# x + b_o of a batch by a broadcast of b_o and a transfer that adds x to it, in place of GpSimd's additions

## The chip, the cores and the metric

The kernel runs on one core of a Trainium2 chip. A core has a matrix engine (TensorE, in the profile PE, its weight loads PEld), a vector engine (VectorE, DVE), an activation engine (ScalarE, ACT), a general engine (GpSimd, POOL), a queue engine that only issues transfers (SyncE, SP), and 16 DMA engines. Each engine executes its own instructions in order; semaphores make one wait for another. The metric is the device time of one execution in microseconds; the kernel before takes 791.95 us (median of 3 runs, 791.62 to 792.87).

## The reference

The input x has 16 batches of 512 rows of 256 floats. All arithmetic is float32. One block, attention and then a feed-forward net, each with a residual and a layer norm:

```python
def favor(x):                          # per head of 16 columns
    p = exp(x - max(x)); return p / (sum(p) + 1e-6)
q = favor(split_heads(x @ Wq + bq)); k = favor(split_heads(x @ Wk + bk))
v = split_heads(x @ Wv + bv)
probs = (q @ k.T) / (sum(q) + 1e-6)
attn = merge_heads(probs @ v) @ Wo + bo
x = layernorm(x + attn)

def fp4_linear(x, w): return fp4(x) @ fp4(w).T   # blocks of 16, scale = max|.|/6, 8 magnitudes
h = silu(fp4_linear(x, w_gate)) * fp4_linear(x, w_up)      # 704 columns
out = layernorm(x + fp4_linear(h, w_down))
```

The change concerns one term: the `x + ... + bo` of the first layer norm's argument.

## The kernel before

A batch is four tiles of 128 rows (`TPB = 4`), worked in two pairs of tiles; there are 32 pairs. Attention is linear in k and v: with no softmax over keys, `probs @ v @ Wo` is q times a small matrix, so a batch goes through these steps.

- `load_x` (L394): the batch's x, 512 KB, by SP into a ring of four buffers. The first batch comes in two halves (L400). Right after batch 1's load, SP issues all other weights (`load_rest`, L465 to L475), among them b_o, broadcast to 128 partitions.
- `project`, per pair: PE transposes x (L636), ACT copies the result (L639), PE multiplies by Wq and Wk (L778), DVE adds the bias (L781) and takes the maximum per head (L786), POOL subtracts it (L790).
- `features`, per batch: ACT's exponential (L801), DVE's sums (L803) and reciprocals (L810 to L814), POOL's scaling of the four tiles (L820).
- `key_values`, per batch: DVE sums k (L829), PE multiplies x by k (L836), by Wv (L852, L853) and by Wo (L864), which gives a 256x256 matrix M; ACT copies it (L843, L870).
- `attend`, per pair: PE transposes q (L636), POOL forms `xb = x + b_o` (L885) into a ring of two buffers, PE multiplies q by M (L892). Then `norm`: DVE adds PE's result and xb (L733) and sums, ACT squares (L740, L742), POOL takes the inverse root (L746 to L748), ACT applies (L755). The pair goes to DRAM by ACT's queue (L903).
- `quantise`, `gate_up`, `down`, per pair: the feed-forward net. SP reads the pair back (L910), DVE and ACT make fp4 codes, SP regroups codes and scales through DRAM (L676, L681, L699, L704), POOL multiplies codes by scales (L929, L1009), PE runs the gate and up products (L957) and the down product (L1026), `norm` again, and the output goes by ACT's queue, for the last two pairs by SP's.

The weights of the feed-forward net are quantised by DVE, ACT and POOL (`weight_scales`, `fp4_exact`, L509 to L584) between the attention work of the first batches. `LEAD = 11` makes attention run some 11 batches ahead of the feed-forward net.

Nothing is ordered by hand. Each step is an `op` with an engine, a cost in us, a due time, what it reads and writes, and the ring buffers it takes. `Plan.order` simulates the engines with these costs and emits the steps in the order in which they start there; every engine then executes its instructions in that order, whatever the real times are. Its rule, for one engine:

```python
first = min(t for t, _ in c)
t, o = min(((t, o) for t, o in c if t <= first + 0.02), key=lambda x: (x[1].due, x[1].at))
```

`c` holds the steps that can start, with their earliest start `t`. A step can start when the steps it depends on have ended (0.3 us later, `LAG`, if they are on another engine) and its ring has a free buffer. So a step that can start earlier goes first, and the due time decides among those that can start at practically the same time. A transfer (`dma`) is two steps: the issue on its queue and a step of an engine of its own, `DMA:name`, with the time to landing. An x load costs SP 0.1 there, `load_rest` 0.1; the first x half is given 4.5 us, Wq, Wk and Wv 7.0 us, Wo and b_o 14.0 us from the start. Steps on POOL, and some on DVE, also share one `port` in the plan, one at a time.

Of the kernel before, what the change touches and what calls it, by code (L numbers as in the profile page):

```python
# [14 lines left out]
ALU = mybir.AluOpType  # L15
AX = mybir.AxisListType

P = 128
HD = 16
BLK = 16  # L20

LEAD = 11

FIRST = 2

# [4 lines left out]
PAIR = 25.0  # L30
# [65 lines left out]
class Plan:  # L96
# [7 lines left out]
    def op(self, eng, us, due, fn, ins=(), outs=(), holds=(), table=None, port=None, name=""):  # L104
        o = Op()
        o.eng, o.us, o.fn, o.due, o.table, o.name = eng, us, fn, due, table, name

        o.port = eng == "POOL" if port is None else port
        o.preds, o.succs, o.new, o.bufs, o.end = set(), [], [], [], None
        ins = [x if isinstance(x, tuple) else (x, None) for x in ins]  # L110
        outs = [x if isinstance(x, tuple) else (x, None) for x in outs]
        for b, key in ins:
            for k, w in b.last.items():
                if key is None or k is None or k == key:
                    o.preds.add(w)
        for b, key in outs:
            if b not in o.new:
                o.new.append(b)
            for k, w in b.last.items():
                if key is None or k is None or k == key:  # L120
                    o.preds.add(w)
            for k, rs in b.reads.items():
                if key is None or k is None or k == key:
                    o.preds.update(rs)
        for b, key in ins:
            b.reads.setdefault(key, []).append(o)
        for b, key in outs:
            b.last[key] = o
            b.reads[key] = []
        for b in holds:  # L130
            if b not in o.new:
                o.new.append(b)
        for b in {id(b): b for b in [b for b, _ in ins + outs] + list(holds)}.values():
            b.users += 1
            o.bufs.append(b)
        o.preds.discard(o)
        for p in o.preds:
            p.succs.append(o)
        o.left = len(o.preds)
        o.at = len(self.ops)  # L140
        self.ops.append(o)
        return o
# [103 lines left out]
def t_pe(n):  # L246
    return 2 * (n / 1200.0 + 0.002)
# [19 lines left out]
def tile_favor_fp4_block(  # L267
# [16 lines left out]
    nc = tc.nc  # L284
    B, L, D = hidden.shape
    FF = w_gate.shape[0]
    TPB = L // P
# [30 lines left out]
    op = plan.op  # L318

    def buf(shape, tag, bufs, name, dtype=F32):  # L320
        return Buf(sb, [P] + list(shape), tag, bufs, name, dtype)

    def dma(name, us, due, fn, ins=(), outs=(), queue="SP", issue=0.45, holds=()):

        op(queue, issue, due, fn, ins=ins, outs=outs, holds=holds)
        op("DMA:" + name, us, due, lambda: None, ins=ins, outs=outs)
# [4 lines left out]
    def psum(tag, name):  # L331
        return Bank(share, tag, name)
# [38 lines left out]
    def twice(ap):  # L371

        return ap.unsqueeze(1).to_broadcast([ap.shape[0], 2, ap.shape[1]])
# [9 lines left out]
    def pu(ap):  # L383

        return ap.rearrange("p (u d) -> p u d", u=2)
# [26 lines left out]
    b_o = const.tile([P, D], F32, name="b_o")  # L412
# [27 lines left out]
    def loaded(name, at):  # L440
        b = Fixed(name)
        op("DMA:" + name, at, 0.0, lambda: None, outs=[b])
        return b

    wqkv_in, wo_in = (loaded(n, t) for n, t in (("wqkv", 7.0), ("wo", 14.0)))
# [183 lines left out]
    def transposed(srcs, tag, name, due, src_ins, bufs=2):  # L629

        pt = psum("pt", f"p{name}")
        dst = buf([4, P], tag, bufs, name)

        def tr():
            for j, s in enumerate(srcs()):
                nc.tensor.transpose(pt[:, j, :], s, ident)  # L636

        op("PE", 2 * t_pe(P), due, tr, ins=src_ins, outs=[pt], holds=[dst], name=name)
        op("ACT", t_act(4 * P), due, lambda: nc.scalar.copy(dst.tile, pt.tile), ins=[pt], outs=[dst])  # L639
        return dst  # L640
# [118 lines left out]
        op("ACT", 0.6 * n, due, apply, ins=[(r, key), nb, rstd], outs=[(dst, key)])  # L759


    qks, Ms = {}, {}

    def project(b, p, due):

# [110 lines left out]
    def attend(b, p, due):  # L876
        i = b * PPB + p
        two = slice(2 * p, 2 * p + 2)
        x, qk, M = xs[b], qks[b], Ms[b]
        qT = transposed(  # L880
            lambda: [qk[:, 2 * p + u, c * P : (c + 1) * P] for u in range(2) for c in range(DC)],
            "qT", f"qT_{i}", due, [(qk, 2 * p), (qk, 2 * p + 1)],
        )
        xb = buf([2, D], "xb", 2, f"xb_{i}")
        op("POOL", 1.4, due, lambda: nc.gpsimd.tensor_tensor(xb.tile, x[:, two, :], twice(b_o), ALU.add),  # L885
           ins=[x, wo_in], outs=[xb])
        pa = psum("pm", f"pa_{i}")

        def mm_a():
            for u in range(2):  # L890
                for c in range(DC):
                    nc.tensor.matmul(  # L892
                        pu(pa.tile)[:, u, :], qT[:, 2 * u + c, :], M[:, c, :],
                        start=c == 0, stop=c == DC - 1,
                    )

        r = buf([2, D], "r", 3, f"r1_{i}")
        op("PE", 2 * DC * t_pe(D), due, mm_a, ins=[qT, M], outs=[pa], holds=[r, xb], name="attend")
        x1 = buf([2, D], "x1n", 2, f"x1n_{i}")
        norm(pa, lambda u: xb[:, u, :], x1, f"a{i}", due, [xb], r, lambda u: x1[:, u, :])  # L900

        d = Buf(dr, [P, 2, D], "x1", NP, f"dx1_{i}")
        dma(f"wx1_{i}", 3.0, due, lambda: nc.scalar.dma_start(d.tile, x1.tile), ins=[x1], outs=[d], queue="ACT")  # L903
        st[i] = {"d": d}
# [136 lines left out]
    def due_at(j):  # L1041

        return (j - PPB * LEAD) * PAIR

    T0 = 0.0
    for b in range(B):
        d = due_at(PPB * b)
        load_x(b, d - 6 * PAIR)
        for p in range(PPB):
            project(b, p, d + (p - 3) * PAIR)  # L1050
        features(b, d - PAIR)
        key_values(b, d - 0.8 * PAIR)
        for p in range(PPB):
            attend(b, p, d + (p - 0.5) * PAIR)
# [63 lines left out]
```

## Time and profile before

| | |
|---|---|
| median of 3 runs | 791.95 us (791.62 to 792.87) |
| the profiled execution, its own time | 793.69 us |
| its span in the profile | 792.0 us |
| mean granted clock of PE | 0.995 |
| PE busy | 768.6 us, 97% |
| DVE, POOL, ACT busy | 656.7 us, 455.9 us, 416.5 us |
| DMA packets | 89.23 MB, mean 113 GB/s |
| L885, the additions | 32, mean 1285 ns, 41.0 us, from 15.8 to 392.9 us |

Busy time is what an engine's instructions cover; an instruction that starts before the one ahead of it has ended is counted once. A row of a timeline has the start and the duration in us, engine, line, operation, output and inputs, shapes and count; a bracket at its end gives the idle time before it and what ended that. A list of waits has who waited for whom, the total in us, how many times, and the longest. In the table by stretch, a row has the window, its length, each engine's busy time with the number of instructions, PE's granted clock, the share of the DMA engines' time, and GB/s.

### The profile page before, as it was taken

How to read it: one execution, taken by the hardware profiler on the slowest of the kernel's cores; microseconds unless marked ns; L12 is line 12 of the kernel's file. 1: busy time of each engine (PE TensorE's matmuls, PEld its weight loads, DVE VectorE, ACT ScalarE, POOL GpSimd, SP SyncE). 2: the span in 40 equal slices, each digit the busy share in tenths (PEclk: the TensorE clock that was granted, in tenths of full speed). 3: DMA queues.
4: the chain of work that ended last, by engine and by line, in shares of the span. 5: the costliest groups of instructions: out<-in, count | busy, mean ns of one | idle time of the engine just before them, and what ended most of it. 6: DMA issues, size and time to landing. Idle time of an engine off the chain costs nothing.

```text
span 792.0 us, 10915 instructions
## 1 busy us (share of the span) xinstructions
PE 768.6 (97%) x3118; PEld 552.5 (70%) x3118; DVE 656.7 (83%) x1340; ACT 416.5 (53%) x893; POOL 455.9 (58%) x602
## 2 busy tenths in 40 slices
PE   7999999989998999999999999999999999999996
PEld 3567657657676777767777777777777777777774
DVE  2998999999888798697697798888878988778784
ACT  2347766868887783544545444444334444344441
POOL 5668788889887755574554435434533543543633
PEclk9999999999999999999999999999999999999998
DMA  9112411211111044404335454554554554464441
GB/s 277 45 55 86 142 53 54 82 60 62 54 53 62 30 129 133 118 37 124 100 112 138 145 171 136 152 149 134 149 154 135 145 149 140 125 179 129 136 130 41
DMA packets 104348, 89.23 MB, mean 113 GB/s; under 512 B 44512, under 2 KB 87904, under 8 KB 104288
## 3 DMA queue, kind: packets, MB, share of 16 engines
q1 hardware_dynamic: 90704, 71.49, 31.8%
q10 hardware_dynamic: 13584, 17.04, 6.0%
q8 instruction: 25, 0.41, 0.2%
q14 instruction: 35, 0.29, 0.1%
HBM read 53.28 MB, written 35.21 MB: 112 GB/s over the span
## 4 chain that ended last, share of the span: by engine, by line
PE 62%; DVE 12%; DMA 8%; POOL 8%; issue 4%; ACT 4%; SPq 2%; ACTq 0%; POOLq 0%; DVEq 0%
PE bank L957 26%; PE bank L1026 14%; PE bank L778 8%; PE bank L892 5%; PE bank L836 5%; POOL hq L1009 3%; DMA out_dram<-y 3%; DVE qk L781 2%; PE bank L636 2%; DVE mx L786 2%; DMA hcT<-g_h 2%; SPq L681 1%; POOL xqT L929 1%; DVE fs L803 1%; PE bank L852 1%
## 5 line engine op out<-in xcount | busy, mean ns | idle before, releaser
L957 PE MATMUL bank<-w_guT,xqT 128*128 128x352 f32 x1024 | 311.3, 459 | 0.0
L957 PEld LDWEIGHTS bank<-w_guT,xqT 128*128 128x128 f32 x1024 | 193.8, 190 | 100.4 <-ACT g L962 0.2
L1009 POOL TENSOR_TENSOR hq<-hcT,hq 128x384 f32<-128x384 bf16 x124 | 127.3, 1058 | 179.3 <-DMA hcT<-g_h 101.4
L1026 PE MATMUL bank<-w_dT,hq 128*128 128x256 f32 (+1 forms) x768 | 173.1, 379 | 1.1 <-DVE r L718 1.1
L1026 PEld LDWEIGHTS bank<-w_dT,hq 128*128 128x128 f32 (+1 forms) x768 | 144.9, 190 | 27.5 <-issue 1.9
L778 PE MATMUL bank<-w_qkv,xT 128*128 128x512 f32 x256 | 120.8, 602 | 3.8 <-DVE qk L781 1.9
L964 DVE TENSOR_TENSOR h<-bank,g 128x352 f32<-128x352 f32 x128 | 65.7, 515 | 50.9 <-ACT g L962 24.1
L962 ACT ACTIVATE g<-bank 128x352 f32<-128x352 f32 x128 | 57.6, 458 | 87.7 <-PE bank L957 77.8
L666 ACT ACTIVATE sq<-h,magic 128x704 f32<-128x704 uint16 x64 | 56.2, 878 | 79.2 <-DVE h L663 78.6
L820 POOL TENSOR_TENSOR qk<-qk,fr 128x512 f32<-128x512 f32 x64 | 67.0, 1073 | 20.5 <-DVE fr L814 18.9
L790 POOL TENSOR_TENSOR qk<-qk,mx 128x512 f32<-128x512 f32 x64 | 67.4, 1068 | 19.2 <-DVE mx L786 19.0
L778 PEld LDWEIGHTS bank<-w_qkv,xT 128*128 128x128 f32 x256 | 46.6, 193 | 45.4 <-issue 35.8
L755 ACT ACTIVATE y<-r,nb_d,rstd_d 128x256 f32<-128x256 f32 x60 | 32.6, 591 | 59.2 <-POOL nb_d L748 59.2
L929 POOL TENSOR_TENSOR xqT<-xcT,xs 128x256 f32<-128x256 bf16 x64 | 46.3, 740 | 27.6 <-DMA d_h<-sT_h 23.4
L836 PE MATMUL bank<-qk,x 128*128 128x256 f32 x256 | 59.7, 387 | 2.1 <-ACT qT L639 2.1
L892 PE MATMUL bank<-M,qT 128*128 128x256 f32 x256 | 59.6, 381 | 1.8 <-ACT M L870 1.8
L655 DVE TENSOR_REDUCE bank<-h 128x44 f32<-128x704 f32 x64 | 57.1, 893 | 1.6
L663 DVE SCALAR_TENSOR_TENSOR h<-h,bank 128x704 f32<-128x704 f32 x64 | 56.7, 886 | 2.1
L836 PEld LDWEIGHTS bank<-qk,x 128*128 128x128 f32 x256 | 49.5, 195 | 12.7 <-ACT qT L639 3.4
L781 DVE TENSOR_TENSOR qk<-bank,b_qkv 128x512 f32<-128x512 f32 x64 | 43.0, 681 | 18.3 <-PE bank L778 17.9
L892 PEld LDWEIGHTS bank<-M,qT 128*128 128x128 f32 x256 | 47.8, 190 | 13.2 <-ACT M L870 3.8
L885 POOL TENSOR_TENSOR xb<-x,b_o 128x512 f32<-128x512 f32 x32 | 41.0, 1285 | 22.8 <-DVE r L733 22.7
(137 smaller groups left out, 1083.3 us busy)
## 6 DMA issues: line engine op xcount, KB each, us to landing
g_h<-hw SPq DMA_DIRECT2D x31, 384.0 KB, 2.8
hcT<-g_h SPq DMA_DIRECT2D x124, 96.0 KB, 2.4
hq<-d_h SPq DMA_DIRECT2D x31, 384.0 KB, 4.1
dx<-x1n ACTq DMA_DIRECT2D x32, 256.0 KB, 2.0
x<-dx SPq DMA_DIRECT2D x32, 256.0 KB, 3.1
x<-_attn_hidden_states_dram SPq DMA_DIRECT2D x15, 512.0 KB, 3.5
out_dram<-y ACTq DMA_DIRECT2D x30, 256.0 KB, 3.3
xs<-d_x SPq DMA_DIRECT2D x32, 128.0 KB, 2.5
```

The lines of the kernel that those rows point to most:

```text
L655: op("DVE", t_dve(n), due, lambda: nc.vector.tensor_reduce(amax[:, g], b3(src()), AX.X, ALU.max, apply_absolute_value=True), ins=[src_b], ...
L778: op("PE", t_pe(D2), due, lambda c=c, u=u, pqk=pqk: nc.tensor.matmul(pqk.tile, xT[:, 2 * c + u, :], w_qkv[:, c, :D2], start=c == 0, stop=c ...
L781: op("DVE", t_dve(D2), due, lambda t=t, pqk=pqk: nc.vector.tensor_tensor(qk[:, t, :], pqk.tile, b_qkv[:, :D2], ALU.add), ins=[pqk], outs=[ ...
L790: op("POOL", t_pool(D2), due, lambda g=g: nc.gpsimd.tensor_tensor(qk3()[:, g, :], qk3()[:, g, :], bcast(mx[:, g], HD), ALU.subtract), ins= ...
L820: nc.gpsimd.tensor_tensor(f3, f3, bcast(r[:, t * 2 * H : (t + 1) * 2 * H], HD), ALU.mult)
L836: nc.tensor.matmul(pxk[:, c * D : (c + 1) * D], x[:, t, c * P : (c + 1) * P], qk[:, t, D:], start=t == 0, stop=t == TPB - 1,)
L892: nc.tensor.matmul(pu(pa.tile)[:, u, :], qT[:, 2 * u + c, :], M[:, c, :], start=c == 0, stop=c == DC - 1,)
L957: op("PE", t_pe(F2), due + u * 0.2 * PAIR, lambda c=c, u=u, lo=lo, ps_=ps_: nc.tensor.matmul(ps_[:, :F2], xqT[:, 2 * u + c, :], w_guT[:, c ...
L962: op("ACT", t_act(F2), due, lambda g=g, pg=pg: nc.scalar.activation(g.tile, pg[:, :F2], AF.Silu), ins=[pg], outs=[g], table="silu")
L964: op("DVE", t_dve(F2), due, lambda g=g, h=h, pu_=pu_, k=k: nc.vector.tensor_tensor(h[:, k * F2 : (k + 1) * F2], pu_[:, :F2], g.tile, ALU.m ...
L1009: op("POOL", t_pool(TG * P), d, lambda u=u, c=c: nc.gpsimd.tensor_tensor(hq()[:, u, :, c, :].rearrange("p g (a t) -> p g a t", t=32), hcT. ...
L1026: op("PE", t_pe(D), due, lambda f=f, g=g, c=c, n=n, u=u: nc.tensor.matmul(pu(pd.tile)[:, u, :], hq()[:n, u, g, c, :], w_dT[:n, f, :], star ...
```

## The change

For batches 2 to 15 the sum x + b_o of the whole batch is made by two transfers into a new ring `xbb` of two buffers of four tiles each. The first, on SP, writes b_o from DRAM to every row of the buffer. The second, on POOL's queue, reads x of the batch from DRAM a second time and adds it to what stands there, so it waits until the first has landed. DVE's L733 then reads the batch's buffer. Batches 0 and 1 keep POOL's additions, in a ring `xb` of one buffer instead of two.

```diff
+SUM = 2
...
-    qks, Ms = {}, {}
+    qks, Ms, xbs = {}, {}, {}
...
-        xb = buf([2, D], "xb", 2, f"xb_{i}")
-        op("POOL", 1.4, due, lambda: nc.gpsimd.tensor_tensor(xb.tile, x[:, two, :], twice(b_o), ALU.add),
-           ins=[x, wo_in], outs=[xb])
+        if b >= SUM:
+
+            if p == 0:
+                xbs[b] = buf([TPB, D], "xbb", 2, f"xbb_{b}")
+                dma(f"bo{b}", 6.0, due - PAIR, lambda: nc.sync.dma_start(
+                    xbs[b].tile, bo.unsqueeze(0).unsqueeze(0).to_broadcast([P, TPB, D])), outs=[xbs[b]])
+                dma(f"xa{b}", 5.0, due - PAIR, lambda: nc.gpsimd.dma_start(
+                    xbs[b].tile, hidden[b].rearrange("(t p) d -> p t d", p=P), accum_op=ALU.add), outs=[xbs[b]],
+                    queue="POOL", issue=1.2)
+            xb = xbs[b]
+            of = lambda u: xb[:, 2 * p + u, :]
+        else:
+            xb = buf([2, D], "xb", 1, f"xb_{i}")
+            op("POOL", 1.4, due, lambda: nc.gpsimd.tensor_tensor(xb.tile, x[:, two, :], twice(b_o), ALU.add),
+               ins=[x, wo_in], outs=[xb])
+            of = lambda u: xb[:, u, :]
...
-        norm(pa, lambda u: xb[:, u, :], x1, f"a{i}", due, [xb], r, lambda u: x1[:, u, :])
+        norm(pa, of, x1, f"a{i}", due, [xb], r, lambda u: x1[:, u, :])
```

The helper that both transfers go through is unchanged:

```python
def dma(name, us, due, fn, ins=(), outs=(), queue="SP", issue=0.45, holds=()):
    op(queue, issue, due, fn, ins=ins, outs=outs, holds=holds)
    op("DMA:" + name, us, due, lambda: None, ins=ins, outs=outs)
```

## The prediction

> **What bounds the kernel now.** I read the page's busy shares first, then PE's waits, then the first 40 us engine by engine, because the change puts new work on two queues whose order is fixed before the kernel runs.
>
> The page's shares, and the list of what PE waited for between 8 and 770 us:
>
> ```profile
> span 792.0 us, 10915 instructions
> PE 768.6 (97%) x3118; PEld 552.5 (70%) x3118; DVE 656.7 (83%) x1340; ACT 416.5 (53%) x893; POOL 455.9 (58%) x602
> ```
> ```profile
> PE bank L836 <- ACT qT L639: 2.1, 1, 2.1
> PE bank L778 <- DVE qk L781: 1.9, 3, 0.8
> PE bank L778 <- ACT xT L639: 1.9, 5, 0.7
> PE bank L892 <- ACT M L870: 1.8, 3, 1.1
> ```
>
> PE is busy 97% of the span; these four lines with the four small ones below them are 10.6 us in all (2.1+1.9+1.9+1.8+1.1+1.0+0.5+0.3). In the table by stretch PE is busy 510.00 of 510 us from 260 to 770. So an early saving counts only as far as it lets PE work denser before 260 us (10.6 us at most), while PE time lost early is nearly all lost: nothing later has room.
>
> Busy time by stretch (columns: PE, weight loads, DVE, ACT, POOL, then clock and DMA share):
>
> ```profile
> 20.00:60.00 40.00, 38.07 (x161) 24.96 (x160) 38.66 (x59) 17.34 (x32) 26.02 (x30) 1.00 0.16 53
> 60.00:240.00 180.00, 173.41 (x779) 123.90 (x778) 165.20 (x310) 134.63 (x293) 152.87 (x192) 1.00 0.22 70
> ```
>
> Until 60 us DVE (38.66 of 40) and PE (38.07) are both full and POOL isn't; from 60 to 240 POOL has 152.87 of 180, 85%, high but not full. DVE's waits for POOL between 20 and 260 us come to 4.6 us (L829 2.0, L569 2.0, L571 0.6).
>
> Now the start, instruction by instruction: POOL, then SP, then DVE.
>
> ```profile
> 4.96 0.34 POOL L491 TENSOR_SCALAR_AFFINE_SELECT mask<-mask 128x128 f32<-128x128 f32 x1
> 13.77 2.08 POOL L790 TENSOR_TENSOR qk<-qk,mx 128x512 f32<-128x512 f32 x2 [8.48 <-DVE mx L786]
> 15.80 1.26 POOL L885 TENSOR_TENSOR xb<-x,b_o 128x512 f32<-128x512 f32 x1
> 17.20 2.08 POOL L790 TENSOR_TENSOR qk<-qk,mx 128x512 f32<-128x512 f32 x2
> ```
> ```profile
> 12.03 0.59 SPq L475 DMA_DIRECT2D wdn<-in_L_ffn_w_down_dram  x1
> 12.67 42.98 SPq L394 DMA_DIRECT2D x<-_attn_hidden_states_dram  x4
> ```
> ```profile
> 23.32 1.22 DVE L786 TENSOR_REDUCE mx<-qk 128x64 f32<-128x1024 f32 x1
> 24.45 2.28 DVE L803 TENSOR_REDUCE fs<-qk 128x128 f32<-128x2048 f32 x1
> 26.64 0.68 DVE L781 TENSOR_TENSOR qk<-bank,b_qkv 128x512 f32<-128x512 f32 x1
> ```
> ```profile
> 19.00:21.00 2.00, 2.00 (x6) 0.94 (x5) 2.00 (x1) 1.69 (x1) 1.51 (x2) 1.00 0.79 258
> 21.00:23.00 2.00, 2.00 (x6) 0.90 (x5) 2.00 (x3) 0.22 (x1) 0.00 (x0) 1.00 0.17 56
> ```
>
> The reader is to see three things. POOL is idle for 8.48 us before its first subtraction (L790), which begins at 13.77. SP sends the loads of x of batches 2 and 3 at 12.67 and about 13.1, behind all the weights; they land 9.3 and 10.2 us later (the two landing times of the DMA list), at 22.0 and 23.3, and only in the last row above does DMA traffic fall away. And DVE's sum of batch 0 (L803, 24.45) follows the exponential, which ACT ran from 19.31 for 1.91 us, to 21.22: its slack is 24.45 - 21.22 = 3.2 us.
>
> **The change part by part.**
>
> *Additions removed.* 28 of the 32 POOL additions go: 28 x 1.285 us (the group's mean) = 36.0 us. Some 20 of them lie in 60-240, 25.7 us.
>
> *Additions by transfer.* 14 POOL issues come. No row shows POOL issuing a transfer; the nearest are ACT's issue of x1n (0.33 us) and POOL's longest instruction, the 128x3072 memset (2.66 us). I take 1.2 us, what the plan charges and close to the addition it replaces (1.27): 14 x 1.2 = 16.8 us; with the ends 4.6 and 37.2. In 60-240 (some 10 batches) POOL then goes from 152.9 to 152.9 - 25.7 + 12.0 = 139.2 us, 77%. That is worth something only where POOL held others: between 0 and the 4.6 us of DVE's waits; as POOL's load falls by a tenth, I take 1.0 us gain.
>
> *A lock between DVE and POOL.* At 102.70 DVE's L813 took 1.09 us against a median of 0.19, while POOL ran L790 (102.68, 1.06 us): one held the other for 0.9 us. The row goes both ways, so POOL's writing of the transfer's rows can be held too, 14 x 0.9 = 12.6 us at most; in the sum it is inside the 2.66 end. The Trainium skill (SBUF — State Buffer, section "SBUF: two separate sides") speaks against this change: a transfer issued from GpSimd writes its descriptors through the port pair it shares with VectorE, and starves while VectorE runs in a two-port mode, about 620 ns becoming 3100. By that rule alone an issue would be an estimated 1.2 + 2.5 = 3.7 us, 14 of them 52 us, more than the additions cost; no row here shows a POOL transfer, and the sum goes by the row.
>
> *Broadcasts on SP.* 14 transfers of 512 KB. An x load of that size issues in 0.38 us and lands in 3.5 (medians). They and the 14 additions move 14.7 MB more beside 89.23 MB, at DMA shares of 0.22 (60-240) and 0.46 (260-770): nothing, hidden by PE, which is full. If a broadcast sat in front of a regrouping load in 260-400 and delayed it, 4 batches x 3.5 us = 14 us is what it could cost without that cover. SP itself is held for up to 22.2 us by a load of x that waits for L836; a broadcast behind such a load is late, and POOL waits for it with all its subtractions and scalings behind. The plan knows these waits, so I put 0, with an end of +4.
>
> *x free sooner.* SP's waits for L885 (6.1 us, 3 times) go; next in line there is L836 (130.6 us). Worth 0: after the start PE never waited for x.
>
> *One xb slot, not two, for batches 0 and 1.* Pair 1's addition can run only after pair 0's L733, which ends at 48.99. POOL is in L820 until 50.43, then the 1.27 us bring it to 51.7; pair 1's L733 ran at 51.37. So +0.3 us (0 to 3 x 1.27 = 3.8).
>
> *The start.* This is where the sum is made. The planner takes, for each engine, whatever can start first; the due time decides only among what can start within 0.02 us. The two slots of the new buffer are empty at the start, so the broadcasts of batches 2 and 3 can go at once. SP's order becomes the four x loads (and the weights), then these two. On the planner's clock SP is free at 0.5, the broadcasts' data ends at 0.95 + 0.3 + 6 = 7.25 and 7.70, and POOL's two additions start at 7.55 and 8.75. POOL's first L790 can start on that clock only at 13.2 (x 4.9, transpose and copy 6.5, weights 7.3, two tiles and their biases 11.7, maximum 12.9). So both POOL transfers are ordered *ahead of* everything POOL does for batch 0. That clock sets only the order; the times are the chip's:
>
> - On the chip the broadcasts queue behind the x load that lands at 23.3. At the 350 GB/s of that stretch 0.52 MB take 1.5 us, so they land at 24.8 and 26.3. Ends: 24.0 for the second if they fill gaps; 29.1 if a broadcast runs at the 180 GB/s of the slowest part of the start (5.4 to 7.8 us, while all DMA engines are busy).
> - POOL's transfer waits for its broadcast, since it adds to what that wrote, and everything on POOL queues behind it. The second starts at 26.3 and ends at 27.5.
> - Then 2.08 + 1.27 + 2.08 us of L790, addition, L790: the exponential starts at 33.0, not 19.31, and L803 at about 34.95, not 24.45: 10.5 us late. Ends: 7.3 (24.0 and 0.33 us an issue) and 14.8 (29.1 and 2.66).
> - Who waits: DVE stands at L803 with every eviction behind it; PE has its 12 L778 matmuls (24.61 to 30.0) and then stops at L636, the transposes of batch 0, which wait for POOL's L820, after L814, after L803. What is late next is PE's L836 and all that follows.
> - DVE has 1.3 us of idle time in 20-60 and PE 1.9, so about 1.0 us is made up.
>
> Sum: +10.5 - 1.0 (made up) - 1.0 (POOL lighter) + 0.3 = +8.8, call it +9. The profiled execution took 793.69 us, its span 792.0 and 1.7 around it, 1.74 above the median of 791.95; the difference is put on the median: **801 us**.
>
> **The rivals.**
>
> *A, faster: the start doesn't wait.* If POOL's first L790 is not behind the two transfers, or the broadcasts are there in time, only the lighter POOL is left: 1.0 to 4.6 us, 787.4 to 791, say 789.5. The point that decides is 13.77 + 3.2 = 17.0 us: a first L790 up to then costs nothing. For it: POOL has 8.48 idle us there. Against: DMA is full until 20 us.
>
> *B, far slower: POOL becomes the bound.* At 2.66 us an issue, and 2 us of waiting for each broadcast, a batch costs POOL 4.7 us where it saves 2.6. Ten batches: 152.9 + 21 = 174 of 180 us, 97%; with the start's 14.8 and some 6 us of holds, 812 to 816. Against: POOL's 27 idle us in that stretch would have to go first.
>
> *C, the start is late but most is made up*, by a changed order of the later work that fills PE's 10.6 us of waits: +1 to -1, about 792. Against: these waits are short ones behind DVE and ACT, which run as late as PE.
>
> **How the numbers follow.** Main case 0.66, its own range 797 to 806 (7.3 - 1.0 - 1.0 = +5.3 to 14.8 - 1.0 + 0.3 = +14.1, the ends both unlikely at once); A 0.16; B 0.11; C 0.07. A measurement of this kernel tells 0.2%, 1.6 us, from no change. Faster: A and a little of C, 0.18; same 0.06; slower 0.76. The range reaches to most of A below and, above, to where B begins: 790 to 811.
>
> **What would show it.** Right: the POOL rows of the first 30 us begin, after L491, with two transfers, the second at 25 to 28; first L790 near 27.5; L803 near 35 with some 10 us of DVE idle before it, ended by ACT; PE idle of about 10 us near 30 to 40; the PE total of busy time unchanged and the span longer by as much. Wrong: a first L790 before 17 (A); POOL over 95% busy in 60-240 (B); span equal in spite of a late L803 (C). The forecast fails if the order on POOL is another than I read from the planner's rule, or if the broadcasts overtake the weights.

## The result, and the profile after

The changed kernel takes 840.36 us (median, 839.47 to 840.68) beside 791.88 us for the kernel before on the same chip: a ratio of 1.061 (95% interval 1.059 to 1.063), 48 us slower. The forecast was 801 us. In the code of after, a line of before up to about 800 stands two lines later (L790 is L792, L803 is L805), and the later ones 14 or 15 (L885 is L899, L892 is L907, L957 is L972); the broadcast is L890 and the adding transfer L892.

Ahead of everything else, the page's span and busy times:

```profile
span 839.0 us, 10952 instructions
PE 781.2 (93%) x3118; PEld 555.6 (66%) x3118; DVE 663.0 (79%) x1340; ACT 416.1 (50%) x893; POOL 440.7 (53%) x588
```

The span is 47.0 us longer. PE's busy time grew by 12.6 us for the same 3118 matmuls, so a part of the loss is a slower PE (mean clock 0.974 instead of 0.995) and the rest is an idle one. POOL, which the change relieves, is 15.2 us lighter.

The start, in the timelines of POOL, SP, ACT, DVE and PE:

```profile
28.42 1.49 POOL L892 DMA_DIRECT2D xbb<-_attn_hidden_states_dram  x1 [23.11 <-DMA xbb<-in_L_attn_bo_dram]
34.83 1.29 POOL L892 DMA_DIRECT2D xbb<-_attn_hidden_states_dram  x1 [4.92 <-DMA xbb<-in_L_attn_bo_dram]
35.61 2.60 POOL L792 TENSOR_TENSOR qk<-qk,mx 128x512 f32<-128x512 f32 x2
```
```profile
12.42 1.61 SPq L396 DMA_DIRECT2D x<-_attn_hidden_states_dram  x2
14.07 2.64 SPq L890 DMA_DIRECT2D xbb<-in_L_attn_bo_dram  x2
```
```profile
41.47 1.91 ACT L803 ACTIVATE qk<-qk 128x2048 f32<-128x2048 f32 x1 [24.26 <-POOL qk L792]
43.29 1.05 ACT L641 COPY xT<-bank 128x512 f32<-128x512 f32 x2
```
```profile
43.42 2.29 DVE L805 TENSOR_REDUCE fs<-qk 128x128 f32<-128x2048 f32 x1 [20.10 <-ACT qk L803]
```
```profile
43.91 7.53 PE L780 MATMUL bank<-w_qkv,xT 128*128 128x512 f32 x12 [19.13 <-ACT xT L641]
```

POOL's first work after the masks is the two adding transfers, and each waits for its broadcast. They go 6.4 us apart: 512 KB in 6.4 us is 82 GB/s, where the prediction took 350. The first subtraction (L792) follows at 35.61 instead of 13.77, the sum L805 at 43.42 instead of 24.45. ACT's exponential (L803) waits 24.26 us for POOL, and the copies of the transposed x (L641) that PE needs for its next 12 matmuls stand behind it in ACT's order. So PE stands still for 19.13 us, and the 12 matmuls then take 7.53 us; in the kernel before the same 12 (L778) waited 0.29 us and took 5.42.

What PE waited for longest over the whole span (us in total, times, longest):

```profile
PE bank L780 <- ACT xT L641: 25.1, 5, 19.1
```

Before, this wait was 1.9 us (L778).

Busy time by stretch (columns: PE, weight loads, DVE, ACT, POOL, then PE's clock, DMA share and GB/s):

```profile
20.00:60.00 40.00, 20.87 (x80) 12.54 (x79) 19.45 (x28) 8.28 (x10) 20.37 (x19) 0.74 0.35 62
60.00:240.00 180.00, 162.07 (x686) 112.80 (x685) 155.71 (x280) 109.52 (x244) 124.83 (x160) 0.96 0.47 103
23.50:25.50 2.00, 1.28 (x9) 0.80 (x7) 0.00 (x0) 0.00 (x0) 0.00 (x0) 1.00 0.31 81
25.50:27.00 1.50, 0.00 (x0) 0.00 (x0) 0.00 (x0) 0.00 (x0) 0.00 (x0) 1.00 0.85 75
30.00:40.00 10.00, 0.00 (x0) 0.00 (x0) 0.00 (x0) 0.00 (x0) 5.17 (x6) 0.50 0.78 122
```

PE does 20.87 us of work in 20-60, where it did 38.07, and 162.07 in 60-240, where it did 173.41. So the loss isn't the start alone: L957 began at 223.4 and L972 begins at 268.1, 44.7 us late, some 20 of which were lost by 55 us. POOL is busy 124.83 of 180 us in 60-240; it is no bound. From 23.5 to 27 us the broadcasts run, and no adding transfer has been issued yet. They move 81 and then 75 GB/s, while the DMA engines are 31% and then 85% occupied; in the kernel before 79% went with 258 GB/s (19 to 21 us). So their pace hardly depends on how occupied the engines are. In the last row PE's clock is 0.50; its 78% and 122 GB/s hold the adding transfers too.

The DMA list (KB each, median us from issue to landing):

```profile
x<-_attn_hidden_states_dram SPq DMA_DIRECT2D x15, 512.0 KB, 7.2
xbb<-in_L_attn_bo_dram SPq DMA_DIRECT2D x14, 512.0 KB, 9.2
xbb<-_attn_hidden_states_dram POOLq DMA_DIRECT2D x14, 512.0 KB, 6.7
```

A broadcast lands in 9.2 us, and the x loads, which the change doesn't touch, in 7.2 us instead of 3.5.

### The profile page after: what moved, and what is told of

Same layout as the page of the kernel before. It is cut to its first block, busy times and chain, and to the rows that moved or that the text cites. A ratio compares the mean times of both kernels' runs of the same rounds, so it can differ in the third digit from the quotient of the medians.

```text
span 839.0 us, 10952 instructions
## 1 busy us (share of the span) xinstructions
PE 781.2 (93%) x3118; PEld 555.6 (66%) x3118; DVE 663.0 (79%) x1340; ACT 416.1 (50%) x893; POOL 440.7 (53%) x588
## 4 chain that ended last, share of the span: by engine, by line
PE 66%; DMA 11%; DVE 10%; POOL 5%; issue 3%; ACT 2%; SPq 2%; ACTq 0%; POOLq 0%; DVEq 0%
PE bank L972 29%; PE bank L1041 16%; PE bank L780 8%; DMA xbb<-in_L_attn_bo_dram 5%; PE bank L907 4%; PE bank L838 4%; DMA xs<-d_x 1%; PE bank L638 1%; POOL hq L1024 1%; PE bank L866 1%; SPq L683 1%; DVE xc L670 1%; DVE ks L831 1%; DMA g_x<-xw 1%; POOL qk L792 1%
## 5 line engine op out<-in xcount | busy, mean ns | idle before, releaser
L972 PE MATMUL bank<-w_guT,xqT 128*128 128x352 f32 x1024 | 311.8, 459 | 1.3 <-DVE h L979 1.3
L972 PEld LDWEIGHTS bank<-w_guT,xqT 128*128 128x128 f32 x1024 | 193.6, 190 | 102.0 <-DVE h L979 1.7
L1024 POOL TENSOR_TENSOR hq<-hcT,hq 128x384 f32<-128x384 bf16 x124 | 125.5, 1042 | 222.1 <-DMA hcT<-g_h 82.7
L780 PE MATMUL bank<-w_qkv,xT 128*128 128x512 f32 x256 | 131.0, 645 | 29.7 <-ACT xT L641 25.1
L780 PEld LDWEIGHTS bank<-w_qkv,xT 128*128 128x128 f32 x256 | 49.6, 205 | 77.4 <-issue 39.0
L668 ACT ACTIVATE sq<-h,magic 128x704 f32<-128x704 uint16 x64 | 56.3, 879 | 82.9 <-DVE h L665 81.0
L792 POOL TENSOR_TENSOR qk<-qk,mx 128x512 f32<-128x512 f32 x64 | 71.5, 1217 | 7.0 <-DVE mx L788 7.0
L907 PE MATMUL bank<-M,qT 128*128 128x256 f32 x256 | 61.0, 385 | 1.6 <-DVE wpr_g L584 1.6
L907 PEld LDWEIGHTS bank<-M,qT 128*128 128x128 f32 x256 | 49.3, 194 | 17.8 <-issue 6.3
L838 PE MATMUL bank<-qk,x 128*128 128x256 f32 x256 | 58.0, 379 | 1.7 <-DVE r L735 1.7
L805 DVE TENSOR_REDUCE fs<-qk 128x128 f32<-128x2048 f32 x16 | 36.4, 2273 | 23.1 <-ACT qk L803 23.1
```

The lines of the kernel that those rows point to most:

```text
L780: op("PE", t_pe(D2), due, lambda c=c, u=u, pqk=pqk: nc.tensor.matmul(pqk.tile, xT[:, 2 * c + u, :], w_qkv[:, c, :D2], start=c == 0, stop=c ...
L792: op("POOL", t_pool(D2), due, lambda g=g: nc.gpsimd.tensor_tensor(qk3()[:, g, :], qk3()[:, g, :], bcast(mx[:, g], HD), ALU.subtract), ins= ...
L838: nc.tensor.matmul(pxk[:, c * D : (c + 1) * D], x[:, t, c * P : (c + 1) * P], qk[:, t, D:], start=t == 0, stop=t == TPB - 1,)
L907: nc.tensor.matmul(pu(pa.tile)[:, u, :], qT[:, 2 * u + c, :], M[:, c, :], start=c == 0, stop=c == DC - 1,)
L972: op("PE", t_pe(F2), due + u * 0.2 * PAIR, lambda c=c, u=u, lo=lo, ps_=ps_: nc.tensor.matmul(ps_[:, :F2], xqT[:, 2 * u + c, :], w_guT[:, c ...
L1024: op("POOL", t_pool(TG * P), d, lambda u=u, c=c: nc.gpsimd.tensor_tensor(hq()[:, u, :, c, :].rearrange("p g (a t) -> p g a t", t=32), hcT. ...
```

## The experiments

All times are in us over the kernel before on the same chip, worked out as (ratio - 1) x 792, with the ratio's 95% interval; the medians of before were 791.4 to 793.1. The expectations speak of differences of medians, which lie up to 1.6 us from these (8.5 there is 6.9 here).

| run | what differs | us over before |
|---|---|---|
| the changed kernel | | 48.2 (46.7 to 49.6) |
| e1_late_first | first two broadcasts late | 29.1 (27.2 to 30.9) |
| e2_sbuf_source | broadcast from SBUF | 20.0 (17.6 to 22.4) |
| e3_both | both | 6.9 (4.5 to 9.2) |
| e4_distinct_rows | 512 different rows | 20.4 (17.7 to 23.1) |
| e5_no_add | both, no adding transfers | 1.7 (0.3 to 3.2) |
| e6_order_only | both, no transfers at all | 2.1 (0.7 to 3.3) |
| e9_free_pool | before, 28 additions left out | -0.6 (-1.7 to 0.5) |
| e15_one_slot | all batches by addition, one slot | 7.2 (5.7 to 8.7) |
| e10_quarter | both, a quarter of each row added | 8.7 (6.4 to 11.0) |
| e11_long_rows | both, rows of 4 KB | 5.9 (4.0 to 7.7) |
| e8_told | both, planner told other times | 4.8 (3.6 to 5.9) |
| e7_act_queue | e1, broadcasts on ACT's queue | 39.1 (37.4 to 40.9) |
| e12_act_later | e1, twelve of them on ACT's queue | 28.0 (26.2 to 29.7) |
| e13_no_lock | both, another kind of DVE instruction | 1.0 (-0.2 to 2.2) |
| e14_no_lock_before | before with that instruction | -0.3 (-1.3 to 0.8) |
| e16_after_no_lock | the changed kernel with it | 37.3 (35.6 to 39.0) |
| e17_late_no_lock | e1 with it | 16.6 (14.4 to 18.8) |
| e18_sbuf_no_lock | e2 with it | 13.6 (11.6 to 15.6) |

### The start and the slow broadcast

Theory: the loss is the start, S (two adding transfers ahead of POOL's first work), and the slow broadcasts all along, R. The rival was that the adding transfers cost by themselves. Four kernels mend the one or the other. The late start is mended by a larger cost of the broadcast in the plan, which moves the two adding transfers behind POOL's first subtractions:

```diff
-                dma(f"bo{b}", 6.0, due - PAIR, ...
+                dma(f"bo{b}", 30.0 if b < 4 else 6.0, due - PAIR, ...
```

> Edit: the changed kernel, where the planner is told that the broadcasts of batches 2 and 3 take 30 us instead of 6. On POOL the two transfers then stand behind all of batch 0's and 1's first subtractions; nothing else is reordered. Theory S+R (the loss has two parts: the start, where POOL's queue stands behind two broadcasts, some 19 us, and later slow broadcasts that hold up SP's and POOL's queues, some 25 us): the start's part goes, 818 to 824 us, first exponential near 19.5 instead of 41.5. Rival A (the adding transfer itself or POOL's lighter or heavier load makes the loss, the start is made up later): 836 to 842. Rival B (the start is all of it): 790 to 796.

Measured: 822.1 us, as S and R together expected. POOL's first L792 is back at 13.3 us and L805 at 23.7, and L972 still begins 23 us late.

```diff
-                    xbs[b].tile, bo.unsqueeze(0).unsqueeze(0).to_broadcast([P, TPB, D])
+                    xbs[b].tile, b_o.unsqueeze(1).to_broadcast([P, TPB, D])
```

> Edit: the changed kernel, where the broadcast reads b_o from its tile in SBUF (128 partitions, each its own row) and not 512 times the one row in DRAM; order unchanged on every engine. Theory S+R with the one DRAM row as what makes a broadcast slow (9.2 us median to landing, against 3.5 for a load of x before): landing falls to 3.5 to 4.5 us, the second broadcast of the start lands near 26, POOL's first subtraction near 28, the total 800 to 806 us. Rival A (a broadcast of 512 KB is slow from anywhere, or the adding transfers hold the DMA engines): landing stays over 7 us, total 834 to 842.

Measured: 813.2 us, above the 800 to 806 expected: a third cost is in it. The broadcast itself lands in 3.4 us, and the x loads come down from 7.2 us to 4.7, by this kernel's DMA list (x loads and broadcasts; the adding transfers stay at 6.4):

```profile
x<-_attn_hidden_states_dram SPq DMA_DIRECT2D x15, 512.0 KB, 4.7
xbb<-b_o SPq DMA_DIRECT2D x14, 512.0 KB, 3.4
```

> Both edits at once: broadcasts of batches 2 and 3 ordered late on POOL, and b_o read from SBUF. Theory S+R: neither part of the loss is left, and what remains is what the removed additions are worth: 787 to 793 us. Rival A (POOL's adding transfers, 1.35 us each, and their traffic cost by themselves): 797 to 815.

Measured: 801.6 us, a miss: S and R mended, some 7 us stay, and the rival had said that they would.

Whether the source in DRAM is slow, or the one row that 512 packets read, is told by a source of 512 different rows in DRAM:

```diff
-                    xbs[b].tile, bo.unsqueeze(0).unsqueeze(0).to_broadcast([P, TPB, D])
+                    xbs[b].tile, hidden[b].rearrange("(t p) d -> p t d", p=P)
```

> Edit: the changed kernel, where the transfer in the broadcast's place reads the 512 rows of x of the batch from DRAM instead of 512 times the row b_o; same size, same place, same order. (It leaves b_o out for batches 2 to 15 and adds x twice.) If it is the one row that is slow: landing 3.5 to 4.5 us after the start, total within 3 us of the kernel with b_o from SBUF, 798 to 808. If reading 512 KB more from DRAM there is slow whatever the rows: landing over 7 us and total 834 to 842.

In the DMA list, the transfer that stands for the broadcast:

```profile
xbb<-_attn_hidden_states_dram SPq DMA_DIRECT2D x14, 512.0 KB, 3.6
```

It lands in 3.6 us and costs what the SBUF source costs (20.4 and 20.0). So the slow one is the read of one row, not DRAM; why the chip reads one row slowly, no run here shows.

### What the rest of it isn't

Theory T puts the remaining 7 us on the adding transfers, rival O on the plan's other order and the one xb slot. Both edits of e3 stay in; the transfers become empty functions, so that the planner orders everything else as before:

```diff
-                dma(f"xa{b}", 5.0, due - PAIR, lambda: nc.gpsimd.dma_start(...
+                dma(f"xa{b}", 5.0, due - PAIR, lambda: None, ...
```

> Leaves out the 14 adding transfers (batches from the third on get b_o without x); the broadcast comes from SBUF and the first two come late as in the experiment with both edits (801.6 us, 8.5 above the kernel before on its chip), and the order of all other work is that experiment's. Theory T, the 8.5 us are the adding transfers' own (14 issues of 1.35 us on POOL, slower POOL instructions behind them, 7 MB through the DMA engines): 0 to 3 us above the kernel before. Rival O, they are the plan's order and the one slot left for xb: 7 to 9.5 us above the kernel before. Between the two: both have a part.

> Leaves out broadcasts and adding transfers both (batches from the third on add b_o's own tile, without x); the order of all other work is that of the experiment with both edits. What is left over the kernel before is the order's and the one slot's alone, less what 28 additions taken off POOL bring. Theory T: within 2 us of the run without the adding transfers, and -2 to 3 us against the kernel before. Rival O: 7 to 9.5 us above the kernel before. Rival B, broadcasts from SBUF still cost SP's queue and the DMA engines something: 3 to 8 us below the run without the adding transfers.

Measured: 1.7 and 2.1 us. T holds: some 5 of the 7 us are the adding transfers'. B falls: with and without the broadcasts from SBUF the time is the same within the intervals. And in e6 POOL has 28 additions less and nothing in their place, and the kernel isn't faster. That is tested by itself in the kernel before:

```diff
-        op("POOL", 1.4, due, lambda: nc.gpsimd.tensor_tensor(xb.tile, ...
+        op("POOL", 1.4, due, lambda: b < 2 and nc.gpsimd.tensor_tensor(xb.tile, ...
...
-        norm(pa, lambda u: xb[:, u, :], ...
+        norm(pa, lambda u: xb[:, u, :] if b < 2 else b_o[:, :], ...
```

> The kernel before, with its own plan, order and two xb slots; only the 28 additions of x and b_o for the batches from the third on are left out (these batches add b_o without x), and nothing stands in their place. It prices the relief of POOL alone. The prediction's term: 1.0 us faster than the kernel before (0 to 4.6). Rival: POOL's additions lie wholly beside PE's work and the relief is worth nothing, -0.3 to 0.3 us; then the 2.0 us of the run without any transfer are the plan's order and the one slot. If the relief is 4 us or more, the order and the slot cost 6 us or more.

Measured: -0.6 us, and its interval holds zero. By relieving POOL the change could not win more than about 1.7 us here, however cheap its transfers were.

```diff
-SUM = 2
+SUM = 99
```

> The changed kernel with its transfers never used (all batches add x and b_o on POOL, as before): what is left of the change is the one xb slot instead of two. The prediction's term: +0.3 us (0 to 3.8). If the 1.8 to 2.0 us of the runs without adding transfers are the slot's: 1 to 3 us above the kernel before. If they are the plan's other order alone: -0.5 to 0.8 us.

Measured: 7.2 us, outside both expectations. But here all 32 additions share the slot (POOL waits 26.7 us for L735 to free it, 22.7 before); in the changed kernel only four do. The run doesn't price the slot there; e5 and e6, with four additions on it, bound slot and order together to about 2 us.

### What in the adding transfers costs

POOL's time for the issue (theory P), or the bytes in the DMA engines (rival D)? One run keeps the rows and cuts the bytes, the other keeps the bytes and cuts the number of pieces:

```diff
-                    xbs[b].tile, hidden[b].rearrange("(t p) d -> p t d", p=P), accum_op=ALU.add)
+                    xbs[b].tile[:, :, : D // 4], hidden[b].rearrange("(t p) d -> p t d", p=P)[:, :, : D // 4], accum_op=ALU.add)
```

> As the experiment with both edits (8.5 us above the kernel before on its chip; without the adding transfers 1.8), but each adding transfer adds a quarter of every row: as many rows for POOL to describe, 128 KB moved instead of 512 (three quarters of x are left out of the sum). Theory P, the 6.7 us are POOL's: the issue of 1.35 us and the slower instructions behind it stay, and so does the time, 7 to 9.5 us above the kernel before. Rival D, they are the 512 KB in the DMA engines, late x loads and late transfers beside them: 2 to 4 us above.

```diff
-                    xbs[b].tile, hidden[b].rearrange("(t p) d -> p t d", p=P), accum_op=ALU.add)
+                    xbs[b].tile, hidden[b].rearrange("(p t) d -> p t d", p=P), accum_op=ALU.add)
```

> As the experiment with both edits, but the adding transfer reads 4 KB in one piece for each partition (rows of x land in other places, so the sum is of other rows) instead of four pieces of 1 KB: the same 512 KB in a quarter of the pieces. Theory P: if the issue on POOL falls with the number of pieces (0.35 to 0.7 us instead of 1.35), 2 to 5 us above the kernel before. Rival D: the bytes are the same, 6.5 to 9.5 us above, unless the landing also falls below 5 us.

The adding transfer's issue on POOL, by its line (ns, least, median, most), first with a quarter of the bytes, then with long rows:

```profile
L892 POOL DMA_DIRECT2D xbb<-_attn_hidden_states_dram x14: 1297/1347/1820, 38.3 to 357.7; - x14
```
```profile
L892 POOL DMA_DIRECT2D xbb<-_attn_hidden_states_dram x14: 872/924/1203, 38.2 to 356.6; - x14
```

A quarter of the bytes saves nothing (8.7 us), so D falls. With a quarter of the pieces the issue takes 0.92 us instead of 1.35, less of a fall than I had expected, and the total is 5.9 us, between the two bands and within e3's interval, so that this run decides nothing. P is left by e10 alone, and not as a price by itself: 14 x 1.35 = 18.9 us of issues take the place of 36.0 us of additions, whose removal was worth nothing.

The planner may simply have counted on wrong times:

```diff
-                dma(f"bo{b}", 6.0, ...    dma(f"xa{b}", 5.0, ...   issue=1.2)
+                dma(f"bo{b}", 30.0 if b < 4 else 4.0, ...    dma(f"xa{b}", 7.0, ...   issue=2.0)
```

> As the experiment with both edits (broadcast from SBUF, first two late; 8.5 us above the kernel before), but the planner is told the measured times: the broadcast's landing 4.0 us instead of 6.0, the adding transfer's 7.0 instead of 5.0, and 2.0 us of POOL's time for its issue instead of 1.2. If the residual is a plan that counts on wrong times: 0 to 5 us above the kernel before. If it is the transfers' own: 6.5 to 10 us above it.

Measured: 4.8 us, in the first of the two bands but not near zero; the order differs too, and e3's interval begins at 4.5, so this run doesn't settle it.

### How the slow broadcast costs: one queue, or all

Theory H: transfers stand behind the broadcast in SP's queue. Rival E: it holds the DMA engines that all queues share. The broadcast goes to ACT's queue, with the planner left as it was:

```diff
-                dma(f"bo{b}", ..., lambda: nc.sync.dma_start(
+                dma(f"bo{b}", ..., lambda: nc.scalar.dma_start(
```

> As the experiment that sends the first two broadcasts late (822.1 us, 29.1 above the kernel before on its chip), but the slow one-row broadcast is issued from ACT's queue; the order of everything else is the same. Theory H, the 20.6 us that the slow broadcast costs there are transfers that stand behind it in SP's queue: xs, g_x, xcT and the x load land in their old times (x load under 5 us instead of 7.1), and the total is 9 to 16 us above the kernel before (ACT pays some 0.4 us an issue, and x1's writes stand behind it now). Rival E, the broadcast holds the DMA engines for all queues: the landing times stay long and the total is 23 to 30 us above the kernel before.

Measured: 39.1 us, above both bands. On ACT's queue nothing holds the first two back: they go at 2.4 us, before the weights have landed, and the first exponential starts at 29.71 instead of 18.86. The run can't be read against e1, so it was repeated with the first two on SP's queue:

```diff
-                dma(f"bo{b}", ..., lambda: nc.sync.dma_start(
+                dma(f"bo{b}", ..., lambda: (nc.sync if b < 4 else nc.scalar).dma_start(
```

> As the experiment that sends the first two broadcasts late (29.1 us above the kernel before on its chip), the first two broadcasts from SP's queue as there, the other twelve from ACT's queue: the same start, and no slow broadcast in SP's queue after it. Theory H, transfers that stand behind the broadcast in SP's queue: 9 to 16 us above the kernel before, x loads land in under 5 us. Rival E, the broadcast holds the DMA engines that all queues share: 25 to 31 us above, x loads land in 6.5 us or more. The run with all fourteen on ACT's queue had its start 10.8 us later than the one it was compared with, which is more than its total was above (9.5).

Its x loads, from the DMA list:

```profile
x<-_attn_hidden_states_dram SPq DMA_DIRECT2D x15, 512.0 KB, 6.8
```

The kernel is 28.0 us over before, and the x loads on SP's queue are as late as with the broadcast in front of them (the twelve broadcasts on ACT's queue land in 8.6 us). H falls. The same trace shows the hold itself. A broadcast goes out on ACT's queue at 80.28 us, an x load on SP's queue at 81.82; from 82 to 86.5 us, of all queues, only ACT's (q10) moves packets, and the x load lands 10.0 us after its issue:

```profile
q10 hardware_dynamic: 354, 0.36, 47.9%
x<-_attn_hidden_states_dram SPq DMA_DIRECT2D x1, 512.0 KB, 10.0
```

This is E as far as the other queue's transfer is held up. That the engines are full isn't so: their packets cover 47.9% of that stretch. What holds the other transfers back, no run here shows.

### The last 7 us: a wait of VectorE

The traces of the kernels with adding transfers have one DVE row that the others haven't. In the kernel with both edits, DVE and then POOL, around 195 us:

```profile
194.80 4.49 DVE L670 TENSOR_SCALAR xc<-sqx 128x512 uint16<-128x512 uint16 x1
```
```profile
190.02 1.35 POOL L892 DMA_DIRECT2D xbb<-_attn_hidden_states_dram  x1
190.90 1.57 POOL L822 TENSOR_TENSOR qk<-qk,fr 128x512 f32<-128x512 f32 x1
191.92 1.29 POOL L574 TENSOR_TENSOR wxm_g<-wxm_g,wdn 128x352 f32<-128x352 f32 x1
192.66 3.58 POOL L822 TENSOR_TENSOR qk<-qk,fr 128x512 f32<-128x512 f32 x3
195.71 2.54 POOL L792 TENSOR_TENSOR qk<-qk,mx 128x512 f32<-128x512 f32 x2
197.75 1.25 POOL L569 TENSOR_TENSOR wpr_g<-wxm_g,wdn 128x352 f32<-128x352 f32 x1
```

The shift of x1's codes (L670, L668 before) takes 0.42 us as a rule and 4.49 here; one more, at 148.1 us, takes 3.29. POOL works without a gap from the adding transfer's issue on until 199.00, and the shift ends at 199.29. The kernel before never shows more than 1.17 us for it:

```profile
L668 DVE TENSOR_SCALAR xc<-sqx x32: 379/418/1173, 77.6 to 733.9; 128x512 uint16<-128x512 uint16 x32
```

All 32 shifts take 18.2 us there, 26.9 in the changed kernel (longest 4.47), 25.1 with both edits, 19.1 without the adding transfers. The planner keeps a common `port` for POOL's work and this shift (`port=True`) and leaves a gap on POOL for it; the issue is in its books with 1.2 us and takes 1.35. That these 0.15 us close the gap isn't shown: in e8 the plan has 2.0 us for the issue, and one shift still takes 4.32 us. (The record of the issue overlaps that of the next POOL instruction, which looks 0.5 us longer for it; by the ends it is 1.3 to 1.4 us in all, and the "slower instructions behind it" in my expectations are that overlap.)

The test keeps the order and changes the kind of the instruction; the control is the same edit in the kernel before:

```diff
-            dst[:, at : at + n], lower(sq()), 6, None, ALU.logical_shift_left), ins=[sq_b],
+            dst[:, at : at + n], lower(sq()), 6, None, ALU.logical_shift_left) if n > 2 * D else nc.vector.tensor_reduce(dst[:, at : at + n], lower(sq()).unsqueeze(2), AX.X, ALU.max), ins=[sq_b],
```

> As the experiment with both edits (8.5 us above the kernel before on its chip), in the same order, but VectorE's instruction that shifts the codes of x1 (xc, 32 of them, 0.42 us each where nothing holds them, 3.29 and 4.49 us where POOL runs several instructions in a row behind an adding transfer's issue) is a reduction over one element, a kind that shows one duration everywhere in the traces; the shift is left out. Each costs VectorE some 0.26 us more (0.68 for a reduction of as many elements). To be read against the same edit on the kernel before. Theory L, POOL late by the issue's extra 0.15 us and the 0.65 us of the instructions behind it meets VectorE's shift, which then waits for POOL's whole run, and the 6.7 us are these waits: 0 to 3 us above that control. Rival Q, POOL's lateness reaches the softmax chain by itself: 6 to 9 us above the control.

> The kernel before with the reduction over one element in place of the shift of x1's codes (the shift is left out), same order: the control of the run above. In the kernel before the shift never took over 1.17 us, so both theories expect -1 to 4 us against the kernel before: at most 32 x 0.26 = 8.3 us more on VectorE, most of it beside PE's work.

With both edits and this kind of instruction, its line (ns, least, median, most):

```profile
L671 DVE TENSOR_REDUCE xc<-sqx x32: 642/647/692, 76.4 to 731.5; 128x512 uint16<-128x512 uint16 x32
```

1.0 us over before, control -0.3: theory L. Every instruction is 0.23 us longer than an unhindered shift, and the kernel 5.9 us shorter than with the shift; its two long waits were 6.9 us beyond the usual. The Trainium skill ("SBUF — State Buffer", section "SBUF: two separate sides") calls the port pair of GpSimd and VectorE an exclusive lock that the first to start holds for its whole instruction. The runs agree that a kind of instruction decides, and differ in the length: the shift waited here for at least four POOL instructions in a row, until POOL's first gap.

### The three terms, one by one

The same instruction, last, in the changed kernel and in the kernels with one edit, so that the terms stand without that wait:

> The changed kernel, same order, with the reduction over one element in place of the shift of x1's codes (the shift is left out). The changed kernel was 47.3 us above the kernel before. Theory S, the three terms (start, slow broadcast, lock) add up: 37 to 41 us above the kernel before. Rival C, the slow broadcast's late transfers cover the lock's waits: 44 to 48 us.

> As the experiment that sends the first two broadcasts late (29.1 us above the kernel before on its chip), same order, with the reduction in place of the shift. Theory S: 19 to 23 us above the kernel before, all of it the slow broadcast's. Rival C: 26 to 30 us.

> As the experiment with the broadcast from SBUF and nothing else mended (20.1 us above the kernel before on its chip), same order, with the reduction in place of the shift. What is left is the start alone, POOL's first work behind two adding transfers that wait for full-rate broadcasts. Theory S: 10 to 13.5 us above the kernel before; the prediction's own sum for the start was 10.5 less 1.0. Rival C: 17 to 20 us.

Measured: 37.3, 16.6 and 13.6 us. The first is S and the last 0.1 over the edge of it; 16.6 is below both bands, since the wait was worth 12.5 us beside the slow broadcasts (29.1 - 16.6), more than alone (5.9). It is also more than the two long shifts of e1 (4.20 and 4.48 us); why, no run here shows. The sum, each term with its runs:

| term | from | us |
|---|---|---|
| order, slot, what else is left | e13 | 1.0 |
| the start, broadcasts at full rate | e18 - e13 | 12.6 |
| the one-row broadcasts, start in order | e17 - e13 | 15.6 |
| the two together at the start | e16 - e18 - e17 + e13 | 8.1 |
| DVE's wait for POOL | the changed kernel - e16 | 10.9 |
| | | 48.2 |

The terms add up to 48.2 by the way they are formed; what the runs add is their sizes. Each difference carries 2 to 3 us of its runs' intervals, the one of four runs 3.6. The start's 12.6 can be read off e18's trace: PE waits 10.57 us where it had 0.29, and its 12 matmuls then take 8.08 us instead of 5.42, which makes 12.9.

```profile
34.95 8.08 PE L780 MATMUL bank<-w_qkv,xT 128*128 128x512 f32 x12 [10.57 <-ACT xT L641]
```

In the changed kernel the same two numbers are 19.13 and 7.53, which makes 20.9: the start with slow broadcasts, 12.6 + 8.1 = 20.7 in the table.

Of the one-row broadcasts' 15.6, some 12.6 show in 60-240. There the kernel of e17 does 161.92 us of PE work, that of e13 174.48:

```profile
60.00:240.00 180.00, 161.92 (x692) 112.58 (x691) 150.64 (x287) 122.02 (x273) 131.11 (x171) 0.97 0.52 113
```
```profile
60.00:240.00 180.00, 174.48 (x776) 124.74 (x775) 164.24 (x314) 135.61 (x304) 144.02 (x188) 1.00 0.47 124
```

The waits for transfers in e17 between 60 and 260 us show where some of it goes:

```profile
POOL xbb L892 <- DMA xbb<-in_L_attn_bo_dram: 10.5, 3, 4.0
POOL xqT L944 <- DMA d_x<-sT_x: 7.7, 1, 7.7
```

POOL stands before an adding transfer, with the softmax work behind it, until the broadcast has landed; and it waits once for a small transfer that regroups x1's scales. In e13 the only such wait in that stretch is 3.1 us.

## Why the prediction was wrong

The direction, and the first step, were right: the planner put POOL's two adding transfers ahead of its first subtraction. What failed is the price of a broadcast, taken from ordinary transfers, both at the start (the two start terms 20.7 us instead of 9.5) and after it (15.6 us instead of nothing), and the wait between VectorE and POOL, which stood in no sum (10.9 us). Step by step:

- *The start, +10.5 less 1.0 made up.* The order, and the chain from broadcast to POOL to exponential to L803, came as written. With a broadcast at full rate its numbers nearly hold: e18's L805 starts at 34.45 and e2's first L792 at 27.99; I had 34.95 and 27.5. Two sizes failed, and one wait. "At the 350 GB/s of that stretch 0.52 MB take 1.5 us" was 6.4 us, so that the second landed at about 34.8 and not 26.3, outside the 29.1 of my worst end. And nothing was made up; instead PE ran its next matmuls slowly (+2.7 us in e18). "PE has its 12 L778 matmuls (24.61 to 30.0) and then stops" was wrong: PE stopped before these 12, since ACT's copies of the transposed x stand behind the late exponential, and did them at 43.91 us. The start cost 12.6 + 8.1 = 20.7 us, not 9.5.
- *Broadcasts on SP, "nothing, hidden by PE, which is full".* This failed most: 15.6 us. The cost was priced like an x load, by bytes, and PE's fullness was taken for a cover in a stretch where PE is fed by POOL and ACT, which wait for transfers. "14 us is what it could cost without that cover" is near by luck: it was for 260-400 and for transfers behind a broadcast in SP's order, and the loss came in 60-240 and not through that order (e12).
- *The lock, inside an end.* The row that showed it (L813, 1.09 us) was read as 0.9 us that could also hold POOL's descriptor writing, and left out of the sum. DVE was held, not POOL's issue, on another DVE instruction and for 3 to 4.5 us at once: 10.9 us. My bound of 12.6 us, made for POOL's issues, was over it, but it stood inside the 2.66 us end of an issue and not beside it. The starvation of descriptors that the Trainium skill ("SBUF — State Buffer", section "SBUF: two separate sides") names isn't seen: no issue took over 1.83 us in any run, against the estimated 3.7.
- *POOL's issues, 14 x 1.2 us.* Measured 1.35.
- *Additions removed, 1.0 us (0 to 4.6).* Measured 0.6 (-0.5 to 1.7).
- *One xb slot, +0.3 (0 to 3.8).* Not settled alone; with the order not over about 2 us.
- *"The PE total of busy time unchanged".* Wrong: +12.6 us, for the same matmuls at a mean clock of 0.974 instead of 0.995.
- *Rivals.* A needed a first L790 by 17.0; it came at 35.6. B needed a full POOL in 60-240; it had 69%, and the time went beyond B's 812 to 816. C, with next to nothing lost, is out.

The range was too low above because every upper end was made from the rates of ordinary transfers, and because the terms after the start were put at or near zero, with covers that weren't tested one against the other.

## What to carry to other kernels

Price a transfer by its access pattern, not by its bytes: a broadcast that reads one row of DRAM hundreds of times took 6.4 us for 512 KB and held up a transfer of another queue, and the same from SBUF cost nothing measurable once the start was in order. Before an engine is relieved, ask whether its work is on the path at all: 36 us less of POOL were worth 1.7 at most, and perhaps nothing. And where an order is planned around a shared port, a new instruction can close the gap that another engine's instruction needed, and that one then waits for the whole run: look for single long rows of an instruction that is short as a rule.

## What the runs showed of the hardware

- One row of 1 KB in DRAM read by all packets of a 512 KB transfer: 82 GB/s, with the DMA engines 31 to 85% occupied; 512 rows or an SBUF source land in 3.3 to 3.8 us instead of 9.2. With it on ACT's queue, x loads on SP's queue take 6.8 us (median), beside 4.7 with the SBUF source and 3.5 before.
- PE's granted clock was 0.50 in the 10 us in which PE stood, and the next 12 matmuls took 7.53 us instead of 5.42. The Trainium skill ("TensorE: Matmul & The Clock Gate", section "Part 1: The HAM clock gate (the "warmup" mystery)") says that the clock falls to half after an idle window of about 3.4 us and stays there for as long a busy one; the rows agree: the clock is still 1.00 at 25.5 to 27 us, after PE's last work at 24.8, and in the windows 44:48 and 48:52, with PE at work again since 43.91, it is 0.50 and 0.97. A prediction that lets PE stand has to add it (2.1 to 2.8 us here).
- An adding transfer of 512 KB from POOL takes 1.35 us of POOL with pieces of 1 KB, 0.92 with pieces of 4 KB, and a quarter of the bytes in as many pieces also takes 1.35. The 512 KB land in 5.8 to 6.7 us.
- A 16-bit shift on VectorE took up to 5.6 us (e7 and e12), until POOL's run of instructions ended, while a reduction over the same data never took more than 0.70.
